# Group 0's first set of products on x as loaded, with paced loads and a later conversion

## The chip, the cores and the metric

The kernel runs on one core of one Trainium2 chip. The metric is the device time of one execution, in microseconds (us). Three runs of the kernel before gave 512.93, 513.04 and 513.55, median 513.04. A core has TensorE (PE, matmuls), VectorE (DVE), ScalarE (ACT), GpSimd (POOL) and SyncE (SP, which here only issues DMA transfers). All data is float32.

## The reference

The input x has 2 x 1024 rows of 512. Every row is normalised, then goes two ways: through a masked linear layer, and through a gated feed-forward with 1792 inner features whose output gates the first.

```
xn = (x - mean) / sqrt(var + 1e-5)                    # per row of 512
s  = xn @ (weight * blockmask).T                      # 512 x 512, blocks of 32 x 32
nx = xn * rsqrt(mean(xn^2) + 1e-5) * ln_w
h  = silu(nx @ gate_w.T) * (nx @ up_w.T)              # 1792 inner features
g  = silu(h @ down_w.T)
out = x + s * g
```

## The kernel before, in words

**Seven products in two levels.** Every large product is done with a Strassen-like scheme: a product of 2 x 2 blocks takes 7 instead of 8 block products, with sums and differences of the blocks before and after. It is applied twice. The outer level (q = 1 to 7, in the order `OUTER`) splits the work into 7 sets; the inner level (m = 1 to 7) makes each set out of 7 products of a 128 x 128 weight by a 128 x 512 operand. A product appears in the profile as two matmul records.

**Groups and instances.** The gate and up weights form 7 groups g (128 rows of each half of both); an eighth group, `G`, is the masked linear layer. One pair (g, q) is an *instance* j of 7 products (`instance`, L333). The order is first (g, 1) and (g, 2) for all groups, then the other five sets of each. So instance 0 is group 0, q = 1; instance 1 is group 0, q = 2; instances 2 and 3 are group 1, q = 1 and 2. The sets q = 1 and 2 use the first 1024 tokens (token tiles t = 0 and 1, of 512 tokens); q = 1 uses features 0 to 255 (chunks c = 0, 1), q = 2 features 256 to 511 (c = 2, 3). The down projection follows the same way at the end (L591).

**An order written out by hand.** `at(pos, fn)` puts a step into one list that is sorted by `pos`; the steps are then issued in that order, so each engine's order, and that of the DMA queue on SP, is the order of the positions. A position is 0.86 us, one product. Instance j's products stand from 7j on; `EARLY` overrides some of the first. `T(us)` turns a planned time into a position. Each engine runs its own list in order; semaphores make it wait for what it needs.

**The opening.** SP loads four x tiles of 128 tokens for t = 0 (`load_x`, L121), the first weight blocks (`load_a`, L251), x for t = 1, and so on. One GpSimd copy (L685) holds the first weight load until the first x tile has landed. For t = 0 and then t = 1: VectorE makes mean and variance per token (`stats`, L125 and L126), `factors` makes scale and shift from them (VectorE, a square root on ACT, VectorE), `normalise` applies them to the four tiles, half on ACT (L148) and half on VectorE (L146), `transpose` turns 128 x 128 blocks on TensorE into PSUM banks (L155), and `evacuate` copies a bank of 128 features x 512 tokens to memory (`raw`, L163). Those are the operands m = 1, 2, 3 of an inner product; m = 5, 6, 7, 4 are differences of them (`inner_b`, L97, since all additions are made by the helper `add`). On the weight side `scale_a` multiplies a block by `ln_w` (L262 on GpSimd, L264 on ACT) and `inner_a` makes four sums of its 128 x 128 blocks. Until the first real transpose, TensorE multiplies the identity by itself (`warm`, L702, 26 products).

**Within an instance.** Products accumulate in PSUM banks X, Y, Z (`PSB`: 3, 2 and 1 of them, V has 2). `seed`, `snap` and `total` copy partial sums out or add them up: from the bank, with the sums of an earlier instance (`prior`) if there is one. For group 0, instance 0 writes its four results to `acc`, instance 1 adds to them and gives the first quadrant of gate and up, `c1`. `silu` (ACT) and `h_out` (VectorE) make h from it, at position `SILU` = 26.2 at the earliest. The `acc` tiles go out to `acc_dram` for the later sets (L466) at 15 positions after the instance's start, and come back before them (L467). The kernel is started in `kernel`, which lays out the arrays; `x_t` is x transposed, used for the final addition only.

Of the kernel before, what the change touches and what calls it, by code (L numbers as in the profile page):

```python
# [31 lines left out]
def tile_masked_linear_gated_ffn(  # L32
# [19 lines left out]
    h_dram = tc.dram_tile([7, G, 2, P, W], F32, name="h_dram")  # L52
    s_dram = tc.dram_tile([KC, NTT, P, W], F32, name="s_dram")
    rms_dram = tc.dram_tile([NT], F32, name="rms_dram")
    acc_dram = tc.dram_tile([G + 1, P, 4, W], F32, name="acc_dram")
    dw_dram = tc.dram_tile([4, P, G, 256], F32, name="dw_dram")

# [45 lines left out]
    ident = const.tile([P, P], F32, tag="ident", name="ident")  # L103
    blockones = const.tile([P, P], F32, tag="blockones", name="blockones")
    keep = const.tile([P, 4, 16], F32, tag="keep", name="keep")

    def constants():
        make_identity(nc, ident)
        nc.gpsimd.memset(blockones, 0.0)
        for b in range(P // BLK):  # L110
            nc.gpsimd.memset(blockones[b * BLK : (b + 1) * BLK, b * BLK : (b + 1) * BLK], 1.0)


    xt, raw, stat = {}, {}, {}
    agg = small.tile([P, NTT, TT, 2], F32, tag="agg", name="agg", bufs=1)
    rms = small.tile([P, NTT, TT], F32, tag="rms", name="rms", bufs=1)

    def load_x(t):
        for i in range(TT):
            xt[t, i] = mem[:, first_slot[("B6", "vc", "v5", "B4")[t]] + i, :]  # L120
            nc.sync.dma_start(xt[t, i], x[(t * TT + i) * P : (t * TT + i + 1) * P, :])  # L121

    def stats(t, i):
# [4 lines left out]
    def factors(t):  # L128


        scl = small.tile([P, TT], F32, tag="scl", name=f"scl_{t}")
        nb = small.tile([P, TT], F32, tag="nb", name=f"nb_{t}")
        stat[t] = (scl, nb)

        def last():
            nc.vector.reciprocal(scl, scl)
            nc.vector.scalar_tensor_tensor(nb, agg[:, t, :, 0], -1.0, scl, ALU.mult, ALU.mult)

        return [lambda: nc.vector.tensor_scalar(scl, agg[:, t, :, 1], 1.0 + EPS, EPS * EPS, ALU.mult, ALU.add),
                lambda: nc.scalar.activation(scl, scl, AF.Sqrt), last]  # L140
# [168 lines left out]
        k = keep[:, 2 * R + K, :].unsqueeze(2).to_broadcast([P, 16, BLK])  # L309
        nc.gpsimd.tensor_tensor(v, v, k, ALU.mult)  # L310

    def inner_a(g, part, k0=0, n=2):

        if part == 1:
            i, si, qs = F["a1"] + 2 * (g % 3), F["s"] + 2 * (g % 2), (1, 2)
        else:
            i, si, qs = *w_slots(g), BLOCKS
        a, s = slots(i + k0, n), slots(si + k0, n)
        a11, a21, a12, a22 = (a[:, :, k * P : (k + 1) * P] for k in range(4))
        s1, s2, s3, s4 = (s[:, :, k * P : (k + 1) * P] for k in range(4))  # L320
        for k in range(n):
            aop[g, qs[k0 + k]] = {1: a11[:, k], 2: a12[:, k], 3: s4[:, k], 4: a22[:, k],
                                  5: s1[:, k], 6: s2[:, k], 7: s3[:, k]}
        return [lambda: add(pool, s1, a21, a22), lambda: add(pool, s2, s1, a11, ALU.subtract),
                lambda: add(pool, s4, a12, s2, ALU.subtract), lambda: add(pool, s3, a11, a21, ALU.subtract)]

    def weights(g, q, m):
        if q < 3 and m in (1, 2, 4):
            return aq[g, 0, q - 1][:, {1: 0, 2: 2, 4: 3}[m] * P :][:, :P]
        return aop[g, q][m]  # L330


    def instance(j, g, q, prior, dest, after):  # L333
# [1 line left out]

        st = {}

        seeded = j > 1

        def mm(m, tag, key, first):  # L340
            if first and key not in st:
                st[key] = bank("Y" if key == "z" and j == 1 else tag, f"{key}_{j}")
            nc.tensor.matmul(st[key], weights(g, q, m), operand(q, m), start=first and not (key == "z" and seeded),  # L343
                             stop=True, skip_group_check=True)

        def seed():

            if seeded:
                st["z"] = bank("Z", f"z_{j}")
                nc.scalar.copy(st["z"], st["x"])  # L350
            else:
                st["s1"] = slot("s2" if j else "s5", f"s1_{j}")
                if prior is None:
                    nc.scalar.copy(st["s1"], st["x"])
                else:
                    add(dve, st["s1"], st["x"], prior(0))
# [15 lines left out]
            else:  # L372
                add(dve, dest(i), st[key], prior(i))

        at(EARLY.get((j, 0), 7 * j + 1), seed)
        for off, m, tag, first, snapshot, out in (
            (0, 1, "X", True, None, None),
            (2, 5, "Y", True, ("s5", 3), None),
# [5 lines left out]
        ):  # L384
            key, pos = tag.lower(), 7 * j + off
            at(EARLY.get((j, m), pos), mm, m, tag, key, first)
            if snapshot:
                at(pos + 1, snap, key, *snapshot)
            elif out:

                pos += 2.3 if prior is None and m == 2 and seeded else 1
                if m == 2:
                    pos = EARLY.get((j, "z"), pos)
                at(pos, total, key, *out)
                after(out[1], pos)


    def group(g, where):
# [39 lines left out]
        def summed(dst, src, into, then=None, engines=(pool,) * 4):  # L438
# [14 lines left out]
            3: (vc, vc, done(0, 1, vc)),  # L453
            4: (acc, acc, done(1, 0, acc)),
        }
        for q in setup:
            instance(where[g, q], g, q, *setup[q])

        def h_sum(q, n, tile_of, a, b):

# [2 lines left out]
            nc.sync.dma_start(h_dram[HD[q], g, n], o)  # L463

        sums, rest = slots(F["acc"] + 4 * (g % 2), 4), 7 * where[g, BLOCKS[0]]
        at(7 * where[g, 1] + 15, lambda: nc.sync.dma_start(acc_dram[g], sums))  # L466
        at(rest - (14 if g else 6), lambda: nc.sync.dma_start(sums, acc_dram[g]))  # L467
        if g < G:
            def again():
# [88 lines left out]
    def load_final(R, Hh, i, slot_s, slot_x):  # L558
# [3 lines left out]
        nc.sync.dma_start(fin[m, t][0], s_dram[m, t])  # L562
        s_tile = fin[m, t][0]
        at_later.append(lambda: nc.gpsimd.tensor_tensor(s_tile, s_tile, rms_bc[t], ALU.mult))  # L564
        nc.sync.dma_start(fin[m, t][1], x_t[m * P : (m + 1) * P, t * W : (t + 1) * W])

    def finish(R, Hh, i, y, pos, eng, part=slice(0, W), source=None):
        r, n = divmod(i, 2)
# [15 lines left out]
    def down_instance(o, q, where_, prior, dest, after):  # L584
# [78 lines left out]
        if last_set:  # L663
            at(where_(17) + 0.1, base_of_last)
            for part, pos in zip(parts, (where_(23), where_(24), where_(25))):
# [8 lines left out]
    where = {gq: j for j, gq in enumerate(order)}  # L674
    N = len(order)
    END = 7 * N
    T = lambda us: (us - 14.0) / 0.86
    EARLY.update({(0, 1): T(10.4), (0, 2): T(11.3), (1, 1): T(12.1), (1, 2): T(13.0), (0, 0): T(11.5), (1, 0): 4.3,
                  (0, "z"): 3.26, (1, "z"): 4.9})
    SILU = 26.2  # L680
    at(T(-10), constants)
    at(T(-10), load_x, 0)
    at(T(-10), lambda: nc.scalar.dma_start(lnw_sb, ln_w))

    at(T(-10), lambda: nc.gpsimd.tensor_copy(mem[:, F["a1"], 0:1], xt[0, 0][:, 0:1]))  # L685
    for K in range(2):
        at(T(-10), load_a, 0, K)
    at(T(-10), load_x, 1)
    for K in range(2):
        at(T(-10), load_a, 1, K)  # L690
    at(T(-10), load_x, 2)
    for K in range(2):
        at(T(-10), load_a, 2, K)
    at(T(-10), load_x, 3)
    def plan(pos, step, todo):
        for i, fn in enumerate(todo):
            at(pos + step * i, fn)
# [3 lines left out]
        for _ in range(n):  # L701
            nc.tensor.matmul(b[:, :P], ident, ident, start=True, stop=True, skip_group_check=True)  # L702

    at(T(1.4), lambda: warm(26, bank("V", "idle")))
    for t, p, step in ((0, T(7.1), 0), (1, T(12.5), 0), (2, 36.0, 1.2), (3, 36.1, 1.2)):
        plan(p, step, factors(t))
    for i in range(TT):
        half = act if i < 2 else dve
        at(T(3.7 + 0.82 * i), stats, 0, i)
        at(T(9.35 + 0.82 * i), stats, 1, i)  # L710
        for h, cols in enumerate((slice(0, W // 2), slice(W // 2, W))):
            at(T(7.95 + 0.9 * h + 0.4 * (i % 2)), normalise, 0, i, half, cols)
            at(T(13.45 + 0.9 * h + 0.4 * (i % 2)), normalise, 1, i, half, cols)
        for c in range(KC):
            at(T((8.9, 9.3, 9.8, 11.0)[c] + 0.05 * i), transpose, 0, c, (2, 3, 0, 1)[i], "XYYX"[c])
            at(T((14.35, 14.8, 15.25, 16.2)[c] + 0.05 * i), transpose, 1, c, (2, 3, 0, 1)[i], "XVVV"[c])
    at(T(6.0), scale_a, 0, 0, pool)
    at(T(6.1), scale_a, 0, 1, pool)
    for c in range(KC):
        at(T((9.75, 10.3, 10.85, 12.05)[c]), evacuate, 0, c, act)  # L720
        at((5.6, T(15.6), 6.0, 3.14)[c], evacuate, 1, c, act)
    for pos, q, m, eng in ((1.1, 1, 5, dve), (1.87, 1, 6, dve), (2.56, 1, 7, dve), (3.95, 2, 5, dve), (2.7, 1, 4, pool),
                           (4.6, 2, 6, dve), (7.2, 2, 7, dve), (5.0, 2, 4, pool)):
        at(pos, inner_b, q, m, eng)
    for q in (1, 2):
        for k in (0, 1):
            for n in (0, 1):
                at(8, outer_b, q, k, n, None)
    at(2.1, scale_a, 1, 0)
    at(5.2, scale_a, 1, 1)  # L730
    for i in range(TT):
        at(14.0 + 2.5 * i, stats, 2, i)
        at(25.0 + 3 * i, stats, 3, i)
        at((44.0, 51.0, 55.2, 58.2)[i], normalise, 2, i, act)
        at(40.5 + 2.4 * i, normalise, 3, i, dve)
    plan(36.2, 1.2, rms_factor())

    for t, p0 in ((3, 51.5), (2, 65.5)):
        n = t % 2
# [21 lines left out]
    for g in range(G + 1):  # L761
        p, rest = 7 * where[g, 1], 7 * where[g, BLOCKS[0]]
        for K in range(2):
# [3 lines left out]
                at(p - (10.4, 7.3)[K], lambda K=K: mask_a(aq[G, 0, K], 0, K))  # L767
            elif g > 1:
                at(p - (10.4, 7.3)[K], scale_a, g, K)
        if g:  # L770
            plan(p - 7, 1, inner_a(g, 1))
        else:
            plan(T(9.9), 0, inner_a(0, 1, 0, 1))
            plan(T(11.9), 0, inner_a(0, 1, 1, 1))
        at(rest - 29, load_block, g)

        def block_sums(g=g):
# [147 lines left out]
```

## Time and profile before

| what | us |
|---|---|
| median of three runs | 513.04 |
| the profiled execution's own time | 513.17 |
| its span, first to last instruction | 511.4 |
| TensorE busy | 505.8 (99%) |
| VectorE busy | 380.4 (74%) |
| GpSimd busy | 340.9 (67%) |
| ACT busy | 182.6 (36%) |
| first real transpose on TensorE starts | 10.16 |
| first product of instance 0 starts | 11.48 |
| first product of instance 3 starts | 31.14 |

All times in the profile are counted from the span's start. A timeline line gives the start, the length, the engine, the line of the kernel, the operation with what it writes and reads, the number of merged instructions, and in brackets how long the engine had been idle and what it had waited for. [...]

### The profile page before, as it was taken

Reading aid. Unit: us, or ns where it says so; the run is one execution under the profiler, and the core shown is the slowest. Engines: PE = TensorE matmul, PEld = TensorE weight load, DVE = VectorE, ACT = ScalarE, POOL = GpSimd, SP = SyncE. Lnnn points to the kernel's source line nnn. Section 1 sums busy time; section 2 is a strip of 40 time slices with the busy share of each in tenths; the row PEclk is TensorE's granted clock in tenths of the full one; section 3 lists DMA queues with packets and bytes.
Section 4 is the critical chain, followed back from the end, with each engine's and each line's share of the span. In section 5 each row is a group of like instructions: output and inputs, shape, how many; then the busy total and the mean of one; then the engine's idle time right before and its main releaser. Section 6 shows DMA issues by size and latency. Waiting matters only on the chain. (4 is left out here: it accounts for less than half of the span.)

```text
span 511.4 us, 4943 instructions
## 1 busy us (share of the span) xinstructions
PE 505.8 (99%) x1269; PEld 231.8 (45%) x1269; DVE 380.4 (74%) x590; ACT 182.6 (36%) x348; POOL 340.9 (67%) x283
## 2 busy tenths in 40 slices
PE   8999999999999999999999999999999999999997
PEld 8444444444444444444444444444444444444444
DVE  6878689876977969699696978968747645367736
ACT  4656754633536353353634433330100101001111
POOL 5522224994795968869597789976662754739960
PEclk9999999999999999999999999999999999999999
DMA  8436636369159386785948667499997698476472
GB/s 289 164 132 238 247 133 227 135 236 350 48 219 348 147 302 228 238 289 208 338 166 294 209 239 254 169 332 383 357 339 270 204 374 327 146 252 216 151 229 83
DMA packets 60460, 121.59 MB, mean 238 GB/s; under 512 B 5760, under 2 KB 13328, under 8 KB 58384
## 3 DMA queue, kind: packets, MB, share of 16 engines
q1 hardware_dynamic: 60288, 121.27, 66.8%
q8 instruction: 10, 0.16, 0.1%
q14 instruction: 18, 0.15, 0.1%
q10 hardware_dynamic: 144, 0.00, 0.0%
HBM read 75.11 MB, written 46.15 MB: 237 GB/s over the span
## 5 line engine op out<-in xcount | busy, mean ns | idle before, releaser
L97 POOL TENSOR_TENSOR mem<-mem 128x512 f32<-128x512 f32 (+4 forms) x245 | 305.2, 1267 | 135.4 <-ACT mem L264 36.5
L343 PE MATMUL x<-mem 128*128 128x512 f32 x448 | 213.6, 595 | 0.2 <-DVE mem L97 0.2
L343 PEld LDWEIGHTS x<-mem 128*128 128x128 f32 x448 | 83.7, 190 | 107.3 <-issue 86.9
L97 DVE TENSOR_TENSOR mem<-x,mem 128x512 f32<-128x512 f32 x137 | 92.5, 684 | 42.0 <-PE x L343 41.1
L343 PE MATMUL y<-mem 128*128 128x512 f32 x224 | 114.5, 593 | 0.3 <-DVE mem L97 0.3
L97 DVE TENSOR_TENSOR mem<-mem 128x512 f32<-128x512 f32 (+3 forms) x60 | 74.7, 1252 | 7.8 <-PE dx L591 4.3
L591 PE MATMUL dx<-mem 128*128 128x512 f32 x174 | 78.3, 592 | 0.0
L97 DVE TENSOR_TENSOR mem<-y,mem 128x512 f32<-128x512 f32 x96 | 65.6, 684 | 9.8 <-PE y L343 8.5
L343 PEld LDWEIGHTS y<-mem 128*128 128x128 f32 x224 | 42.2, 190 | 53.0 <-issue 47.8
L350 ACT COPY z<-x 128x512 f32<-128x512 f32 x54 | 30.9, 573 | 97.9 <-PE x L343 92.2
L343 PE MATMUL z<-mem 128*128 128x512 f32 x112 | 57.3, 593 | 0.0
L591 PEld LDWEIGHTS dx<-mem 128*128 128x128 f32 x174 | 33.1, 190 | 41.6 <-issue 40.4
L591 PE MATMUL dy<-mem 128*128 128x512 f32 x98 | 44.5, 592 | 0.0
L409 ACT ACTIVATE gate<-mem 128x512 f32<-128x512 f32 x56 | 33.1, 601 | 25.3 <-DVE mem L97 20.9
L414 DVE TENSOR_TENSOR mem<-gate,mem 128x512 f32<-128x512 f32 x56 | 38.0, 681 | 5.1 <-POOL mem L97 4.3
L564 POOL TENSOR_TENSOR mem<-mem 128x512 f32<-128x512 f32 x16 | 25.0, 1570 | 15.3 <-DMA mem<-s_dram 15.2
L343 PEld LDWEIGHTS z<-mem 128*128 128x128 f32 x112 | 21.0, 190 | 24.9 <-issue 23.9
L574 ACT ACTIVATE silu<-mem 128x512 f32<-128x512 f32 x15 | 9.0, 602 | 64.6 <-DVE mem L97 48.3
L97 DVE TENSOR_TENSOR mem<-z,mem 128x512 f32<-128x512 f32 x41 | 28.0, 682 | 3.5 <-PE z L343 3.5
L591 PEld LDWEIGHTS dy<-mem 128*128 128x128 f32 x98 | 18.6, 190 | 23.4 <-issue 23.4
L97 DVE TENSOR_TENSOR mem<-dx,mem 128x512 f32<-128x512 f32 x16 | 11.0, 690 | 20.1 <-PE dx L591 20.1
L591 PE MATMUL dz<-mem 128*128 128x512 f32 x56 | 25.2, 592 | 0.0
(73 smaller groups left out, 289.2 us busy)
## 6 DMA issues: line engine op xcount, KB each, us to landing
h_dram<-mem SPq DMA_DIRECT2D x98, 256.0 KB, 2.1
mem<-h_dram SPq DMA_DIRECT2D x28, 768.0 KB, 6.2
mem<-in_gu SPq DMA_DIRECT2D x42, 256.0 KB, 3.7
acc_dram<-mem SPq DMA_DIRECT2D x8, 1024.0 KB, 4.2
mem<-acc_dram SPq DMA_DIRECT2D x8, 1024.0 KB, 6.7
mem<-in_x SPq DMA_DIRECT2D x16, 256.0 KB, 5.2
s_dram<-mem SPq DMA_DIRECT2D x16, 256.0 KB, 4.8
mem<-s_dram SPq DMA_DIRECT2D x16, 256.0 KB, 6.3
```

What stands on the lines that cost most here:

```text
L97: eng.tensor_tensor(o, a, b, op)
L343: nc.tensor.matmul(st[key], weights(g, q, m), operand(q, m), start=first and not (key == "z" and seeded), stop=True, skip_group_check=True)
L350: nc.scalar.copy(st["z"], st["x"])
L409: nc.scalar.activation(gate[key], t(), AF.Silu)
L414: nc.vector.tensor_mul(a(), gate[key], b())
L564: at_later.append(lambda: nc.gpsimd.tensor_tensor(s_tile, s_tile, rms_bc[t], ALU.mult))
L574: nc.scalar.activation(b[0][:, part], y[:, part] if source is None else source(), AF.Silu)
L591: nc.tensor.matmul(st[key], w(), b(), start=first and key != "z", stop=True, skip_group_check=True)
```

## The change

Instance 0 no longer waits for normalised x. Normalising a token is a scale and a shift, so `(x * scale + shift) @ w = scale * (x @ w) + shift * (sum of w over the features)`. The change multiplies the raw `x_t`, loaded already transposed, and converts the four results later.

- **Raw operands.** `x_t` is laid out by chunk and token tile. `raw_x` loads four blocks of 128 features x 512 tokens; `raw_t` makes their differences 5 and 6 on VectorE, 7 and 4 on GpSimd. In `instance`, j = 0 takes these as operands, and its products are planned from 4.6 us on. The first weight block is scaled on ACT and its sums are made on VectorE. `warm` makes 5 instead of 26 idle products.
- **Paced loads.** The first fourteen loads are a list in a fixed order: the weight block for q = 1, four raw blocks, the four x tiles of t = 0, the weight block for q = 2, the four x tiles of t = 1. Loads 3 to 10 of it (counted from 0) each wait for a one-column VectorE copy that reads the tile loaded three places earlier.
- **The order of the opening.** t = 0 is normalised after the raw products, features 256 to 511 first; instance 1 and instances 2 and 3 start around that. The two halves of the weight block of q = 2 are scaled on ACT at 9.8 us in the plan, ahead of the root of `factors` for t = 0. The scaling of group 1's blocks moves from ACT to GpSimd. Position 0 is at 12.2 instead of 14.0 us.
- **Conversion.** `sum_rows` multiplies the scaled weights by a column of ones (the sum over the features). `fac_store` transposes the factors of t = 0 and 1 on TensorE, copies them on ACT, stores them and loads them back broadcast over the partitions. `raw_results` scales and shifts instance 0's results, and adds them to instance 1's: 12 GpSimd operations and 4 on ACT, from position 16 on. `silu` and `h_out` of this quadrant are at fixed positions, 31 and 33 for the first half, 44 and 46 for the second, and the store to `acc_dram` at 46.5.
- A root of a column of ones is taken in `constants`; instance 1 now uses bank Z and instance 2 bank Y; x of t = 1 has other slots; statistics of t = 2 and 3 come a few positions later.

```diff
-    def load_x(t):
-        for i in range(TT):
-            xt[t, i] = mem[:, first_slot[("B6", "vc", "v5", "B4")[t]] + i, :]
+    def load_x(t, *tiles):
+        for i in tiles or range(TT):
+            xt[t, i] = mem[:, (F["B6"], F["B3"] + 2, F["v5"], F["B4"])[t] + i, :]
...
+    def raw_x(k, n):
+        o = rop[k, n] = mem[:, RQ[2 * k + n], :]
+        nc.sync.dma_start(o, x_t[k, n])
+
+    def raw_t(m, eng):
+        b11, b12, b21, b22 = (rop[k, n] for k in (0, 1) for n in (0, 1))
+        o = rop[m] = mem[:, RQ[{5: 4, 6: 5, 7: 6, 4: 7}[m]], :]
+        a, b = {5: lambda: (b12, b11), 6: lambda: (b22, rop[5]), 7: lambda: (b22, b12), 4: lambda: (b21, rop[6])}[m]()
+        add(eng, o, a, b, ALU.subtract)
...
+    def sum_rows():
+        b = bank("V", "row_sums")
+        for r in range(2):
+            for c in range(2):
+                nc.tensor.matmul(b[:, r : r + 1], aq[0, 0, 0][:, (2 * c + r) * P :][:, :P], ones,
+                                 start=c == 0, stop=c == 1, skip_group_check=True)
+        held.append(b)
...
+    def fac_store():
+        b = bank("V", "fac_rows")
+        nc.tensor.transpose(b[: 4 * TT, :P], fac.rearrange("p a t i -> p (a t i)"), ident)
+        rows = small.tile([4 * TT, P], F32, tag="fac_rows", name="fac_rows", bufs=1)
+        nc.scalar.copy(rows, b[: 4 * TT, :P])
+        nc.sync.dma_start(fac_dram.rearrange("a t (i p) -> (a t i) p", p=P), rows)
+        for a in range(2):
+            for t in range(2):
+                nc.sync.dma_start(fac_bc(a, t), fac_dram[a, t].unsqueeze(0).to_broadcast([P, W]))
...
+    def raw_results(p1, c1, silu, h_out):
+
+        tmp = [mem[:, F["B7"] + k, :] for k in range(4)]
+
+        def shift(i):
+            r, n = divmod(i, 2)
+            nc.scalar.mul(tmp[i], fac_bc(1, n), row_sums[:, r : r + 1])
+
+        pos = CONVERT
+        for n in (0, 1):
+            for i in (n, n + 2):
+                at(pos + 0.5, shift, i)
+                at(pos, lambda i=i, n=n: add(pool, p1(i), p1(i), fac_bc(0, n), ALU.mult))
+                at(pos + 1.5, lambda i=i: add(pool, p1(i), p1(i), tmp[i]))
+                at(pos + 3, lambda i=i: add(pool, c1(i), c1(i), p1(i)))
+                pos += 4.5
+            at((31, 44)[n], *silu(n))
+            at((33, 46)[n], *h_out(n))
...
-    T = lambda us: (us - 14.0) / 0.86
...
+    T = lambda us: (us - 12.2) / 0.86
...
+    landing, queue = [], []
+    for o, load in ([(aq_slot(0, 0), lambda: load_a(0, 0))] +
+                    [(mem[:, RQ[2 * k + n], :], lambda k=k, n=n: raw_x(k, n)) for k, n in ((0, 0), (1, 0), (0, 1), (1, 1))] +
+                    [(mem[:, F["B6"] + i, :], lambda i=i: load_x(0, i)) for i in range(TT)] +
+                    [(aq_slot(0, 1), lambda: load_a(0, 1))] +
+                    [(mem[:, F["B3"] + 2 + i, :], lambda i=i: load_x(1, i)) for i in range(TT)]):
+        queue.append((o, load))
+
+    def paced(k):
+        if 3 <= k < 11:
+            dve.tensor_copy(queue[k][0][:, 0:1], queue[k - 3][0][:, 0:1])
+        queue[k][1]()
+
+    for k, us in enumerate((-10, -10, -10, 3.6, 4.2, 4.9, 5.72, 6.52, 7.15, 8.0, 8.8, 8.81, 8.82, 8.83)):
+        at(T(us), paced, k)
...
-    at(T(1.4), lambda: warm(26, bank("V", "idle")))
...
+    at(T(1.4), lambda: warm(5, bank("V", "idle")))
+
+    at(T(4.0), scale_a, 0, 0)
+    for us, m, eng in ((5.75, 5, dve), (6.55, 6, dve), (6.8, 7, pool), (6.7, 4, pool)):
+        at(T(us), raw_t, m, eng)
+    plan(T(4.95), 0, inner_a(0, 1, 0, 1, dve))
+    at(T(10.0), sum_rows)
+    at(T(14.4), lambda: nc.scalar.copy(row_sums, held[0][:, :2]))
+    at(T(18.3), fac_store)
...
+    at(T(9.8), scale_a, 0, 1)
+    plan(T(10.6), 0, inner_a(0, 1, 1, 1))
+    at(T(12.4), scale_a, 1, 0, pool)
+    at(T(12.5), scale_a, 1, 1, pool)
...
-        "x_t": x.reshape(B * S, H).T,
+        "x_t": x.reshape(-1, W, KC, P).transpose(2, 0, 3, 1),
```

## The prediction

> **What bounds the kernel now.** I read the engine table first, then TensorE's waits, its timeline in the first 32 us, the loads, and the busy time by stretches.
>
> ```profile
> PE 505.8 (99%) x1269; PEld 231.8 (45%) x1269; DVE 380.4 (74%) x590; ACT 182.6 (36%) x348; POOL 340.9 (67%) x283
> ```
>
> ```profile
> PE idle L702 <- POOL ident masks.py:199: 1.3, 1, 1.3
> PE y L343 <- DVE mem L97: 0.3, 1, 0.3
> PE x L343 <- DVE mem L97: 0.2, 1, 0.2
> ```
>
> ```profile
> 31.10:503.00 471.90, 471.75 (x1122) 1.00 0.68 241
> ```
>
> TensorE never waits after its first 22 us: from 31.1 to 503 it is busy 471.75 of 471.90 us. So the time is set by when that gapless stretch begins. The mark I use is the first product of instance 3 (group 1, q = 2); what TensorE does from there on is the same in both kernels.
>
> ```profile
> 1.35 8.98 PE L702 MATMUL idle<-ident 128*128 128x128 f32 x52 [1.35 <-POOL ident masks.py:199]
> 10.16 1.47 PE L155 MATMUL pt<-ident,mem 128*128 128x128 f32 x12
> 11.48 1.10 PE L343 MATMUL x<-mem 128*128 128x512 f32 x2
> ...
> 13.72 1.02 PE L343 MATMUL x<-mem 128*128 128x512 f32 x2
> ...
> 31.14 1.45 PE L343 MATMUL x<-mem 128*128 128x512 f32 x3
> ```
>
> A product is two records, 0.86 us from start to start. The mark is at **31.14**. Between 11.48 and 31.14 lie 19 products (16.3 us), 20 transposes at 0.11 (2.2) and 1.1 us of small gaps: this stretch is nearly full too. Only the 9 us of idle products (L702) ahead of it can be used.
>
> ```profile
> 6.00:7.00 1.00, 1.00 (x6) 1.00 1.04 389
> 8.00:9.00 1.00, 1.00 (x11) 1.00 0.95 358
> ```
>
> The columns are the stretch, its length, PE busy (records), granted clock, DMA share, GB/s. TensorE passes 6 idle records in the seventh microsecond and 11 in the ninth; the single records start every 0.213 us until 7.5, every 0.111 after. For 6 us from its first record it ran at half speed, which the PEclk row doesn't show.
>
> [...] The trace has 2.5 to 3.4 for loads not behind a long queue (below). [...]
>
> **The change, part by part.**
>
> *The seven raw products.* The set q = 1 of group 0 (7 products, 6.0 us at full clock, twice that at half) goes to where the idle products were. It needs the first weight block scaled: load landed 3.54 (as the first x load today, issue 0.73), `lnw_sb` landed 3.7, two ACT halves 0.91: first product at 4.8. Five idle products (10 records x 0.213 from 1.45) end at 3.8, so TensorE then idles 1 us and is still cold. [...] (0,1) 4.8, (0,2) 6.5, (0,5) 8.2, (0,6) 9.5, (0,3) 10.4, (0,7) 11.2, row sums 12.1 (four products of one column, 8 records at 0.11 to 0.19; I take 0.9), (0,4) to 13.9[...]. All of it lies before the transposes below, so the cold clock costs nothing unless loads are faster than I take them.
>
> *Paced loads.* From the fourth on, a load waits for a VectorE copy that waits for the landing three loads earlier. So at most three are under way, and one round costs issue to landing plus 0.26 us (0.02 to the copy, 0.18 copy, 0.05 to the issue: today's gate, POOL L685, 3.67 to 3.85, issue at 3.88). What is a landing worth?
>
> ```profile
> L251 SPq DMA_DIRECT2D mem<-in_gu x1: 328/328/328, 3.9 to 3.9; - x1
> ...
> DMA to landing us min/median/max: 3.4/3.4/3.4
> ```
>
> ```profile
> L251 SPq DMA_DIRECT2D mem<-in_gu x6: 332/352/400, 41.6 to 68.3; - x6
> ...
> DMA to landing us min/median/max: 2.5/2.8/3.1
> ```
>
> The first is today's gated load in the opening, 3.4 us; the second is six weight loads with one or two under way, 2.5 to 3.1; the very first x load took 2.8. With three under way I take **2.9**, and keep 2.5 and 3.4 as ends. The new plan's own gate times (3.6, 5.72, 8.0) imply 2.0; no load in this trace was that fast, and the old plan's time for scaling that gated block was 6.0, where the trace has 7.50. Ungated, today's queue lands a load every 0.67 us; gated, three per 3.16, so one per 1.05.
> The chain that matters is loads 0, 3, 6, 9 (load 9 is the block for q = 2): 3.54 + 3 x 3.16 = **13.0**. x's fourth tile (load 8) lands at 11.2, its statistics end at 12.2.
>
> *Behind that landing on ACT.* `scale_a(0, 1)` stands on ACT ahead of the square root and the normalising, so those wait for load 9: two scaling halves (0.82 to the next start), root 0.2, reciprocal and shift on VectorE 0.4: normalising of tiles 0 to 3 starts at 13.0 + 1.5 = **14.5**, where today it starts at 7.8.
>
> *From there (times after 14.5).* ACT: four halves at 0.5, to 2.0, then two evacuations (0.5 apart) end at 2.6 and 3.1. Products (1,1) at 2.7, (1,2) at 3.6 to 4.4; eight transposes to 5.1; evacuation to 5.7; (2,1) 5.75 to 6.6. VectorE meanwhile: two normalisings (0.5 each), four statistics (0.81 each), one total (0.6), ready for the second factors at 5.0; ACT's root comes after the evacuation, 5.6, factors at 6.2. (2,2) 6.6 to 7.5. New here: `fac_store` puts a transpose behind (2,2) on TensorE and its copy on ACT ahead of three of the four normalising halves, so ACT stands from 6.9 to 7.8; the halves run 8.0 to 9.6. Transposes 8.7 to 9.4, first difference on VectorE 0.7, and (1,5) at **9.9**. Then 8 products (6.86), 8 transposes (0.88) and three changes of kind at 0.08 to the mark: 9.9 + 7.9 = **17.8**; 14.5 + 17.8 = **32.3**, against 31.14. That is **+1.2 us**. TensorE idles where it used to be full: the work freed early is paid back as gaps between 14 and 25 us.
>
> *GpSimd's conversion.* 12 additions of 128x512 at 1.28 are 15.4 us, with the four for group 2 (0.73) between them. They can begin once the broadcast factors are in (store about 22.5, 2 us, loads 2.6 more) and the group 1 difference is done, about 29, and end near 47. The later gates (positions 31 and 44) come at about 40 and 52, and the next GpSimd results are needed at 52: 3 us of cover. GpSimd is busy only 2.9 of each 12.8 us there today. I cost it at nothing; each microsecond beyond that cover would be one of TensorE.
>
> *The rest.* Two more ACT copies, four shifts (0.57 each) and VectorE's 8 gates (0.18), two differences (0.68) and four weight sums (0.3) lie where those engines wait anyway. Scaling of group 1 moves from ACT (0.91 a block) to GpSimd (1.86), done by 20, needed at 20. SP's four raw loads add 1 MB of 122; the factor store and its loads hold SP about 2 us near 23, where its next load of today is at 25.5. The final x loads keep packets and size. Banks and slots: nothing.
>
> **Sum.** 513.17 (the profiled execution: span 511.4 and 1.8 around it; 0.13 above the median) + 1.2 = **514.3**. A measurement of this kernel tells about 0.2% (1.03 us, so 512.0 and 514.07) from no change.
>
> **Rivals.**
> *The loads land like today's middle ones*, 2.6 us: load 9 at 12.1, mark at 31.4: 513.4, no change. [...] against: 3.4 in the opening. 0.30.
> *The plan holds*: loads of 2.0 us. Then the clock decides: VectorE's total of (0,7) stands ahead of the reciprocal. With the clock full by 7.5 us, (0,7) ends near 11.2, normalising starts at 12.1, mark 29.9: 511.9, faster. With a switch at 9.1 it starts at 13.2, and nothing is won. 0.18.
> *Every gated load takes 3.4*, as today's: load 9 at 14.5, mark 33.8: 515.8, clearly slower; it decides from 2.8 us a load (mark at 32.04). 0.16.
> My forecast has the other 0.36. GpSimd late by more than its cover would add to any of them.
>
> **How the numbers follow.** Slower by over 0.2%: most of the forecast (0.28), the 3.4 case (0.16), a little of the 2.6 case (0.03): 0.47. Within: 0.36. Faster: 0.17, from the plan's case. The range from 511.7 to 515.9 leaves out about half of each outer case.
>
> **What would show it.** In the new trace: first product near 4.8 and two cold products of 1.7 us; gated loads 2.5 to 3.4 from issue to landing; ACT's scaling of the second block near 13 and the first normalising near 14.5; TensorE idle between 13.9 and 24; the mark at 32.3; no waits after it. I am wrong if loads land in about 2 us, if ACT's normalising doesn't wait for the second block, or if TensorE waits for GpSimd between 40 and 55 us.

## The result and the profile after

The changed kernel takes **516.75 us** (median of four runs, 516.66 to 517.02; the kernel before 513.08 beside them). The ratio is 1.0071 with a 95% interval of 1.0053 to 1.0088: slower by 0.7%, 3.7 us. I had forecast slower by 1.2. The profiled execution took 516.68 us with a span of 514.9, where before it was 513.17 and 511.4.

I split the 3.5 us between the two spans at two points that both kernels have: the mark (first product of instance 3) and the start of TensorE's last matmul record (507.36 and 509.85), called the last product's start below.

| stretch, us | before | after | more | I had predicted |
|---|---|---|---|---|
| start to the mark | 31.14 | 32.87 | 1.73 | 1.2 |
| mark to the start of the last product | 476.23 | 476.99 | 0.76 | 0 |
| start of the last product to the end | 4.03 | 5.04 | 1.01 | not looked at |

**The engine table** answers to the first fence of the prediction: fewer matmuls, the same busy time; ACT and GpSimd do more.

```profile
PE 505.9 (98%) x1236; PEld 227.6 (44%) x1236; DVE 383.0 (74%) x598; ACT 186.5 (36%) x358; POOL 357.4 (69%) x293
```

**TensorE's waits** grow from 1.8 us in three places to 3.9 in seven, all in the opening; the largest:

```profile
PE idle L794 <- POOL ident masks.py:199: 1.4, 1, 1.4
PE x L397 <- DVE mem L98: 0.8, 2, 0.7
PE pt L164 <- ACT mem L157: 0.6, 1, 0.6
```

**TensorE's timeline in the opening**, columns as in the prediction:

```profile
1.38 2.50 PE L794 MATMUL idle<-ident 128*128 128x128 f32 x10 [1.38 <-POOL ident masks.py:199]
4.43 2.06 PE L397 MATMUL x<-mem 128*128 128x512 f32 x2 [0.55 <-ACT mem L273]
6.28 1.92 PE L397 MATMUL z<-mem 128*128 128x512 f32 x2
...
13.46 1.13 PE L397 MATMUL x<-mem 128*128 128x512 f32 x2 [0.66 <-DVE mem L98]
14.71 1.90 PE L164 MATMUL pt<-ident,mem 128*128 128x128 f32 x8
16.49 2.08 PE L397 MATMUL x<-mem 128*128 128x512 f32 x2
18.35 1.24 PE L397 MATMUL z<-mem 128*128 128x512 f32 x2
...
32.87 1.45 PE L397 MATMUL x<-mem 128*128 128x512 f32 x3
```

The raw products run from 4.43, the first two at half speed, as forecast. The forecast's times for them suppose full speed from 9.1 us, an estimate of mine that the trace of the kernel before (full from 7.47) did not show; here it began at 8.54. The product at 16.49 was not forecast like this: from its start to the next is 1.86 us, as at 4.43 (1.85), though TensorE had been at full speed since 8.54. The busy time by stretches shows the granted clock in its fourth column:

```profile
8.40:11.80 3.40, 3.40 (x8) 1.00 0.83 278
11.80:15.20 3.40, 2.62 (x14) 1.00 1.02 269
15.20:18.60 3.40, 3.40 (x9) 0.52 0.86 316
```

For 3.41 us, from 15.37 to 18.78 in the clock record, TensorE was back at half speed. In the 3.41 us before, it had idled about 0.8 us and otherwise done one product, eight products of one column, and transposes.

**ACT at the hand-over** from the loads to the normalising, with the last gated load (the weight block of q = 2) below it:

```profile
12.40 0.91 ACT L273 ACTIVATE mem<-mem,lnw_sb 128x256 f32<-128x256 f32 x2 [1.63 <-DVE st L131]
13.21 0.19 ACT L149 ACTIVATE fac<-fac 128x4 f32<-128x4 f32 x1
13.89 2.08 ACT L157 ACTIVATE mem<-mem,fac 128x256 f32<-128x256 f32 x4 [0.49 <-DVE fac L146]
```

```profile
L260 SPq DMA_DIRECT2D mem<-in_gu x1: 328/328/328, 9.7 to 9.7; - x1
...
DMA to landing us min/median/max: 2.6/2.6/2.6
```

Issued at 9.69, landed at 12.31, scaled at 12.40, normalised from 13.89: the chain of the prediction, 0.6 us earlier. (The scaling's label names VectorE's statistics, which ended at the same moment. In all eight profiles with gates the scaling starts 0.08 to 0.09 us behind load 9's landing.)

**After the mark** the stretch still looks full:

```profile
32.80:504.80 472.00, 471.70 (x1121) 1.00 0.69 243
```

Yet TensorE has two late products, in the timeline around 44 and 56 us. The gaps show in no idle column: a product's records are longer than the distance to the next product (1.02 against 0.86 us at 39.73), so the start-to-start distance must be read.

```profile
42.31 1.88 PE L397 MATMUL x<-mem 128*128 128x512 f32 x4
44.20 1.10 PE L397 MATMUL y<-mem 128*128 128x512 f32 x2
45.14 1.88 PE L397 MATMUL x<-mem 128*128 128x512 f32 x4
```

Two products should take 1.72; here they take 1.89, and the next one 0.94 instead of 0.86. What ACT does just before, and then ACT and the product in the kernel before:

```profile
39.94 0.57 ACT L404 COPY z<-x 128x512 f32<-128x512 f32 x1 [1.13 <-PE x L397]
40.52 1.28 ACT L483 ACT_TABLE_LOAD   x1
41.82 0.60 ACT L483 ACTIVATE gate<-mem 128x512 f32<-128x512 f32 x1
42.35 0.71 ACT L458 ACTIVATE mem<-mem,row_sums 128x512 f32<-128x512 f32 x1
42.97 0.58 ACT L483 ACTIVATE gate<-mem 128x512 f32<-128x512 f32 x1
43.49 0.57 ACT L415 COPY mem<-y 128x512 f32<-128x512 f32 x1
```

```profile
39.21 0.60 ACT L409 ACTIVATE gate<-mem 128x512 f32<-128x512 f32 x1 [0.44 <-DVE mem L97]
39.92 0.58 ACT L361 COPY mem<-y 128x512 f32<-128x512 f32 x1
...
42.30 1.02 PE L343 MATMUL y<-mem 128*128 128x512 f32 x2
```

The copy of bank y (`snap`, L415) must end before the next product into y. Before, it ended at 40.50, and that product came at 42.30. After, four instructions queue back to back ahead of it: the silu's table load (at 32.84 in the kernel before), the silu, a shift copy of the conversion (L458) and another silu. It ends at 44.06, and the product starts at 44.20. The same happens at 56.64 behind the second half's silu. Neither time does ACT wait for GpSimd.

**The tail.** The last two stores of the output, before and after:

```profile
L578 SPq DMA_DIRECT2D out<-mem x2: 403/404/406, 508.3 to 508.8; - x2
...
DMA to landing us min/median/max: 1.7/1.8/1.8
```

```profile
L658 SPq DMA_DIRECT2D out<-mem x2: 332/360/387, 511.1 to 511.6; - x2
...
DMA to landing us min/median/max: 2.4/2.5/2.6
```

They take 0.7 us longer, and the first is issued 0.3 late behind a wait of SP. The trace has an 8 KB transfer of an instruction queue (q14) at 512.5, between issue and landing of both. It ends at 512.9, and only then do the last 18 packets of the stores begin; in each of the seven profiles where this transfer falls on the stores, these packets begin within 0.01 us of its end. SP's wait comes 1.4 us ahead of the transfer. Both come and go together in all profiles, but what ties them is not shown. In the kernel before that transfer came at 512.3, 0.9 us after the span's end.

### The profile page after: what moved, and what is told of

Its sections match the earlier page's. It is cut to its first block, busy times and chain, and to the rows that moved or that the text cites. A ratio compares the mean times of both kernels' runs of the same rounds, so it can differ in the third digit from the quotient of the medians.

```text
span 514.9 us, 4925 instructions
## 1 busy us (share of the span) xinstructions
PE 505.9 (98%) x1236; PEld 227.6 (44%) x1236; DVE 383.0 (74%) x598; ACT 186.5 (36%) x358; POOL 357.4 (69%) x293
## 5 line engine op out<-in xcount | busy, mean ns | idle before, releaser
L98 POOL TENSOR_TENSOR mem<-mem 128x512 f32<-128x512 f32 (+4 forms) x255 | 321.8, 1285 | 124.7 <-ACT mem L425 32.3
L397 PE MATMUL x<-mem 128*128 128x512 f32 x448 | 216.2, 600 | 1.7 <-DVE mem L98 0.8
L98 DVE TENSOR_TENSOR mem<-x,mem 128x512 f32<-128x512 f32 x134 | 90.5, 684 | 38.9 <-PE x L397 38.1
L98 DVE TENSOR_TENSOR mem<-mem 128x512 f32<-128x512 f32 (+2 forms) x66 | 78.3, 1194 | 7.4 <-PE dx L671 4.4
L397 PE MATMUL z<-mem 128*128 128x512 f32 x112 | 58.4, 604 | 0.0
```

Source lines behind the costliest of these rows:

```text
L98: eng.tensor_tensor(o, a, b, op)
L397: nc.tensor.matmul(st[key], weights(g, q, m), operand(q, m) if j else rop[{1: (0, 0), 2: (1, 0), 3: (1, 1)}.get(m, m)], start=first and no ...
```

## The experiments

Each is the changed kernel with one edit or more; ratios are to the kernel before. "Normalising", "mark", "to last" and "tail" are ACT's first normalising half, the mark, the mark to the last product's start, and from there to the end, in the profiled execution.

| kernel | median us | ratio, 95% interval | normalising | mark | to last | tail |
|---|---|---|---|---|---|---|
| the changed kernel | 516.75 | 1.0071 [1.0053, 1.0088] | 13.89 | 32.87 | 476.99 | 5.04 |
| `fill` | 517.37 | 1.0078 [1.0063, 1.0093] | 14.21 | 33.32 | 477.39 | 5.07 |
| `ungated` | 513.96 | 1.0016 [1.0008, 1.0023] | 13.20 | 31.06 | 476.91 | 4.13 |
| `fac_late` | 517.24 | 1.0086 [1.0069, 1.0103] | 14.23 | 32.00 | 477.36 | 5.16 |
| `no_convert` | 515.33 | 1.0044 [1.0029, 1.0059] | 13.83 | 31.69 | 476.24 | 5.18 |
| `pad8` | 516.93 | 1.0072 [1.0057, 1.0087] | 14.91 | 32.78 | 477.20 | 5.10 |
| `ungated_shift` | 513.50 | 1.0004 [0.9996, 1.0013] | 12.93 | 30.79 | 476.51 | 4.13 |
| `ungated_order` | 513.70 | 1.0010 [1.0001, 1.0018] | 13.40 | 31.76 | 476.48 | 4.13 |
| `fill_shift` | 516.81 | 1.0078 [1.0060, 1.0095] | 14.32 | 32.19 | 476.97 | 5.13 |
| `pad_sp` | 515.74 | 1.0042 [1.0027, 1.0057] | 14.76 | 32.63 | 477.23 | 4.12 |
| `ungated_order2` | 512.85 | 0.9990 [0.9983, 0.9998] | 12.12 | 30.43 | 476.52 | 4.14 |
| `ungated_order3` | 513.08 | 0.9997 [0.9990, 1.0004] | 11.92 | 30.13 | 476.50 | 4.13 |
| `after_shift` | 516.55 | 1.0062 [1.0041, 1.0084] | 14.92 | 33.55 | 476.37 | 5.05 |

### `fill`: keep TensorE busy where it idled

```diff
-    at(T(1.4), lambda: warm(5, bank("V", "idle")))
+    idle = []
+    at(T(1.4), lambda: idle.append(bank("V", "idle")))
+    at(T(1.4), lambda: warm(7, idle[0]))
+    at(T(10.05), lambda: warm(5, idle[0]))
+    at(T(10.9), lambda: warm(2, idle[0]))
```

> TensorE is kept from standing idle between the raw set and the first transposes: 7 idle products at the start, 5 more behind the row sums and 2 ahead of the last raw product's successors. If the second half-speed spell (15.2 to 18.6 us) comes from TensorE's idle moments in the window before it, it is gone, and the mark (first product of instance 3) comes about 1.2 us earlier, near 31.7, the time near 515.5. If the spell has nothing to do with idling, or the stretch is bound by VectorE and ACT anyway, the mark stays at 32.9 and the time at 516.7.

Not faster: 517.37. In its profile the clock stays full from 5.68, and (1,1) and (1,2) take their 0.9 us. But the time was not won: in this profile another wait took its place:

```profile
31.11 0.72 ACT L458 ACTIVATE mem<-mem,row_sums 128x512 f32<-128x512 f32 x1 [2.51 <-DMA mem<-fac_dram]
31.73 0.57 ACT L415 COPY mem<-y 128x512 f32<-128x512 f32 x1
```

```profile
32.35 1.12 PE L397 MATMUL y<-mem 128*128 128x512 f32 x2 [0.98 <-ACT mem L415]
```

ACT's first shift copy waits 2.51 us for the broadcast factors. The snap of y stands behind it on ACT, and TensorE waits 0.98 us for the snap. The store of the factors took 3.7 us to land here, 1.4 to 3.1 in the other profiles; in the changed kernel's the same copy waits 0.65 us, and TensorE not at all.

### `ungated`: the loads as one queue

```diff
-        if 3 <= k < 11:
-            dve.tensor_copy(queue[k][0][:, 0:1], queue[k - 3][0][:, 0:1])
...
-    for k, us in enumerate((-10, -10, -10, 3.6, 4.2, 4.9, 5.72, 6.52, 7.15, 8.0, 8.8, 8.81, 8.82, 8.83)):
-        at(T(us), paced, k)
+    for k in range(14):
+        at(T(-10), paced, k)
```

> The eight gates are taken out and all loads are issued in the same order at once. If the gates set the start of normalising (load 9 at 12.3 us), load 9 lands at about 9.7 and the normalising starts 1 us or more earlier; VectorE's total of the sixth raw product, which waits for the cold TensorE until about 12, is then the next bound, so the mark gains 0.8 to 1 us and the time is near 515.8. If the gates help the first loads, the first product (4.43) comes later and nothing is won.

The gates are the largest cost: 2.8 us come back (513.96), more than I expected. The loads land every 0.67 us, load 9 at 10.62 instead of 12.31, and the mark is at 31.06. From normalising to mark it takes 17.86 us. In the profiles 1.8 us of the gain lie ahead of the mark (0.7 an earlier normalising, 1.1 the half-speed spell) and 0.9 in the tail, now 4.13. The gates do not help the first loads: without them the first product starts at 4.36, with them at 4.43.

### `fac_late`: the factor store behind the transposes

```diff
-    at(T(18.3), fac_store)
+    at(T(19.66), fac_store)
```

> The store of the factors, its transpose on TensorE and its copy on ACT come behind the normalising of t = 1 instead of amid it. If ACT's standing there (22.0 to 22.85 us) delays the transposes of t = 1, product (1,5) comes 0.8 us earlier (24.9 to 24.1), and the mark and the time with it (516.0). If the transposes wait for VectorE, nothing changes. The conversion begins up to 1 us later; if GpSimd had no cover, stalls of TensorE between 40 and 57 us would grow.

No gain: 517.24. The first product of t = 1, (1,5), comes 9.0 us after the normalising, where `ungated`, with the old place of the store, has 9.9. But (2,3) then waits 0.45 us for ACT's snap behind the shift copy, as in `fill`, so the stretch to the mark is 17.77. The stretch after the mark is 1.1 us longer than before the change; that is not due to this move, for `fill`, without it, has 1.2.

### `no_convert`: no conversion

It leaves out the conversion: the 12 GpSimd operations and ACT's four shift copies. Instance 1 adds to the unconverted results, and the first quadrant of group 0 comes from them, with silu at its earlier position.

```diff
-            setup.update({1: (None, p1, nothing), 2: (None, c1, nothing)})
+            setup.update({1: (None, p1, nothing), 2: (None, c1, done(0, 0, c1))})
...
-            raw_results(p1, c1, lambda n: (silu, (0, 0, n), lambda: c1(n)),
-                        lambda n: (h_out, (0, 0, n), lambda: c1(n), lambda: c1(n + 2), n))
```

> The 12 GpSimd operations and 4 ACT copies of the conversion are left out, and silu and the product of this quadrant stand at their earlier gates: the first quadrant of group 0 is computed from unconverted results. Only what the conversion and its gates cost is taken away. If the stalls of TensorE after the mark (0.67 us at 44.2, 47.7 and 56.6) come from them, they are gone and the time is near 516.0; if they come from the shifted position of other work, they stay and the time is 516.7.

From the mark to the last product it takes 476.24 us, as before the change (476.23): the whole 0.76 is the cost of the conversion and of the later silu. (The profiles of `pad8` and `pad_sp`, the same kernel up to its end, have 0.97 and 1.00 there.) The opening shows no half-speed spell, and normalising to mark is 17.87.

### `pad8` and `pad_sp`: the tail

```diff
+    pad = small.tile([P, 1], F32, tag="pad", name="pad", bufs=1)
+    for k in range(8):
+        at(END + 40 + 2 * k, lambda: nc.vector.memset(pad, 0.0))
```

> Eight one-column VectorE memsets of an unused tile are added in the last stage; nothing else changes. If the last microsecond (5.0 us from the last product's start to the end, against 4.0 before) comes from an 8 KB instruction fetch that falls on the last stores, because VectorE has eight instructions more than before, eight more move that fetch ahead of the stores, and the stretch is 4.0 to 4.2 again: time near 515.8. If the stores are slow for another reason (the layout of x, the addresses), it stays at 5.0 and 516.8.

Eight more VectorE instructions changed nothing: 516.93, tail 5.10. Then the same with SP, eight transfers of 2 KB:

```diff
+    pad = small.tile([P, 8, KC], F32, tag="pad", name="pad", bufs=1)
+    for k in range(8):
+        at(END + 10 + 3 * k, lambda k=k: nc.sync.dma_start(pad[:, k, :], ln_w))
```

> The changed kernel with eight more small transfers (2 KB each, of the ln_w vector into an unused tile) in SP's queue in the last stage. Eight more VectorE instructions didn't move the last instruction fetch (2.7 us after the last product's start, on top of the last two stores). If it is SP's own instruction stream, which is nine transfers and eight waits longer than before, eight more transfers move that fetch ahead of the last stores' data: the stretch from the last product's start to the end is then 4.0 to 4.2 us again and the time 0.9 us shorter, 515.9. If the fetch is another engine's or isn't the cause, the stretch stays at 5.0.

More work, and 1.0 us faster: 515.74, tail 4.12. No instruction transfer falls on the output stores, and they are quick again. This page counts four stores; the last two landed 1.8 and 1.7 us after their issue.

```profile
L658 SPq DMA_DIRECT2D out<-mem x4: 333/391/406, 509.9 to 511.3; - x4
...
DMA to landing us min/median/max: 1.7/1.9/2.1
```

### `ungated_shift` and `after_shift`: ACT's queue

Shift copies where ACT is free, and the second half's silu, gate product and store later; once on `ungated`, once on the changed kernel as it is.

```diff
-                at(pos + 0.5, shift, i)
+                at({0: 17.1, 2: 20.9, 1: 24.1, 3: 26.1}[i], shift, i)
...
-            at((31, 44)[n], *silu(n))
-            at((33, 46)[n], *h_out(n))
+            at((31, 46.9)[n], *silu(n))
+            at((33, 48.5)[n], *h_out(n))
...
-        at(7 * where[g, 1] + 15 if g else 46.5, lambda: nc.sync.dma_start(acc_dram[g], sums if g else slots(R1, 4)))
+        at(7 * where[g, 1] + 15 if g else 49.0, lambda: nc.sync.dma_start(acc_dram[g], sums if g else slots(R1, 4)))
```

(On `ungated` the first position was 16.5.)

> Without the gates, and with the ACT copies of the conversion at positions 16.5, 20.9, 24.1 and 26.1 (the last at 30 so far), and the second silu, its product and the store behind it 2.5 positions later. If the stalls of TensorE after the mark (0.68 us at positions 34, 38 and 48) come from these ACT steps standing ahead of ACT's copies of product sums, they shrink to 0.1 or less and the time is near 513.3. If they come from GpSimd being late, they stay and the time is 514.0.

> The changed kernel with its gates and its opening, and only ACT's shift copies and the second half's silu, gate product and store at other positions. Theory (the stalls between 44 and 57 us are ACT's queue, with the gates as without them): from the mark to the last product's start about 476.5, where the changed kernel has 476.99, so 0.5 us less: about 516.2. The tail is left as it is, about 5.1. The opening is the same, so the run also tells whether the second half-speed spell belongs to this opening or comes by chance: if it belongs to it, TensorE's clock is at half in some 3.4 us between 15 and 19 again and the first product of instance 3 starts at about 32.9; if it is chance, that product may start at 31.7 (normalising at 13.9 and 17.8 behind it). Rival: the stalls are GpSimd's late conversion, and stay: 477.0 and 516.7.

With all 12 GpSimd operations in place, the stretch after the mark falls from 476.91 to 476.51 on `ungated` and from 476.99 to 476.37 on the changed kernel. So most of the stall is ACT's queue, not GpSimd. The median of `after_shift` moved by less than its interval. In its profile the opening was worse (mark 33.55). Here the half-speed spell came again, from 15.67 to 19.09, after nearly 2 us of waiting in the 3.41 us before:

```profile
13.84 1.13 PE L397 MATMUL x<-mem 128*128 128x512 f32 x2 [1.22 <-DVE mem L98]
15.74 1.97 PE L164 MATMUL pt<-ident,mem 128*128 128x128 f32 x8 [0.77 <-DVE mem L155]
17.53 1.88 PE L397 MATMUL x<-mem 128*128 128x512 f32 x2
```

### `ungated_order`, `ungated_order2`, `ungated_order3`: what an open queue allows

All three start from `ungated_shift`. The first takes VectorE's total of (0,7) behind the factors of t = 0, (0,4) behind it, and lets GpSimd make raw difference 7 ahead of 4.

```diff
-    ... (0, 4): T(10.8), ... (0, ("out", 7)): T(10.68), ...
+    ... (0, 4): T(13.45), ... (0, ("out", 7)): T(12.7), ...
...
-    for us, m, eng in ((5.75, 5, dve), (6.55, 6, dve), (6.8, 7, pool), (6.7, 4, pool)):
+    for us, m, eng in ((5.75, 5, dve), (6.55, 6, dve), (6.6, 7, pool), (6.7, 4, pool)):
```

> As the one before, and VectorE's total of product (0,7) comes behind the normalising of t = 0 instead of ahead of the reciprocal, product (0,4) behind the first transposes, and GpSimd makes the difference that (0,7) needs first. If, with the gates gone, the cold TensorE holds the normalising back through that total, the normalising starts near 11.6 (13.2 so far), the mark comes near 29.5 and the time near 511.8, faster than before the change. If another thing binds (ACT's scaling of the second block, the loads), it gains half a microsecond or nothing.

It missed: the normalising started at 13.40. GpSimd's difference, now at 7.28, fell on VectorE's second one:

```profile
6.57 2.52 DVE L98 TENSOR_TENSOR mem<-mem 128x512 f32<-128x512 f32 x2 [0.73 <-DMA mem<-in_x_t]
9.01 0.68 DVE L131 BATCH_NORM_STATS2 st<-mem 128x6 f32<-128x512 f32 x1
```

```profile
7.28 1.26 POOL L98 TENSOR_TENSOR mem<-mem 128x512 f32<-128x512 f32 x1 [5.16 <-DMA mem<-in_x_t]
```

```profile
6.70 1.42 DVE L98 TENSOR_TENSOR mem<-mem 128x512 f32<-128x512 f32 x2 [0.86 <-DMA mem<-in_x_t]
```

The last fence is `ungated`: the same two differences take 1.42 us there, 2.52 here, and the statistics slide by 1 us. Nothing else differs on VectorE at that time. The one that met GpSimd took 1.79 us, the other 0.69.

The second leaves that swap out, and scales the block of q = 2 on GpSimd (`scale_a, 0, 1, pool`); first shift copy at 17.1. The third adds the edit of `fac_late`.

> As the ungated run with the moved ACT copies (the first now at 17.1), and the total of (0,7) behind the normalising, (0,4) behind the first transposes, GpSimd's two raw differences in their old order (in the run before, the swapped one ran beside VectorE's and made that one 1.1 us longer), and the second block scaled on GpSimd, off ACT's queue. If the total and that scaling held the normalising back once the loads are free, it starts near 11.8 and the mark comes near 29.7: 511.9. If VectorE's statistics bind, it starts at 12.5 and the time is near 512.7. Nothing won at 513.5.

> As ungated_order2, with the store of the factors behind the normalising of t = 1. In the run with that alone, product (1,5) came 0.8 us earlier against the start of the normalising. If that adds up, the mark is 0.6 to 0.8 us ahead of ungated_order2's; if ACT's wait for the factors then stops a product sum, part of it is lost again.

`ungated_order2` is the one version faster than the kernel before: by 0.35 us, 0.10% with an interval of 0.02 to 0.17%. Its normalising starts at 12.12. VectorE makes the factors at 11.21, at once behind its last statistics, so the statistics bind now, and 512.85 is near the 512.7 expected for that case. So the idea is worth a little, once its waits are gone; what each of the edits gave was not separated. `ungated_order3` had a mark only 0.3 us earlier, and its median shows no gain.

### `fill_shift`: are the factors the next bound?

`fill` with the first shift copy at position 17.1, behind the snap of y.

> The kernel with the idle products in TensorE's gaps, and the conversion's first ACT copy moved behind ACT's copy of instance 2's sum, from position 16.5 to 17.1. In the fill run that first copy waited 2.5 us on ACT for the broadcast factors, and product (2,3) waited 1.0 us on TensorE behind it. If that is the second bound under the half-speed spell, the wait of 1.0 us is gone and the mark is near 32.3 (33.3 in fill, 32.9 in the changed kernel). If it is not, the mark stays at 33.3.

The 1 us wait is gone (mark 32.19, and 17.87 from normalising). The median is 516.81, 0.6 below `fill` with overlapping intervals, and not below the changed kernel. So being rid of the spell, which neither filled profile has, did not lower the median; see below.

## Why the prediction was right in direction and short in size

The step that failed is the one from the mark to the end. The prediction moved the mark by 1.2 us and added nothing behind it, since what TensorE does from there on "is the same in both kernels" and the conversion was costed "at nothing". In the profiled execution 1.77 of the missing 2.4 us lie behind the mark: 0.76 in stalls behind ACT and 1.01 in the last stores. The opening was short by 0.57.

**Paced loads: right.** I took 2.9 us a load and 14.5 for the normalising. The three gated loads of the chain took 2.74, 2.73 and 2.63 us, so load 9 landed at 12.31, not 13.0, and the normalising started at 13.89. That is one profile. Over the eight profiles with gates these loads took 2.5 to 3.6 us, mean 2.88, and the start lies between 13.83 and 14.92, mean 14.38. So this profile, with a mean of 2.70, lies nearer to the first rival's 2.6 than to my 2.9, and the eight together do not. What the trace of the kernel before has for that rival is two of its six weight loads between 41 and 69 us, those issued at 67.35 and 68.28, which landed after 2.63 and 2.49. `ungated` confirms that the gates set the normalising's start, though statistics and the total of (0,7) are close behind: there the block lands 1.7 us earlier and the normalising starts only 0.7 earlier.

**From normalising to the mark: right, with an addition.** My 17.8 is 17.86 or 17.87 in the six profiles without a half-speed spell, a factor wait or a reordered total. In the changed kernel's own it was 18.98. In that profile the failing sentence is "the cold clock costs nothing". It looked only at the first switch. TensorE idles behind the gates, as I had written ("TensorE idles where it used to be full"), and the clock falls back for 3.41 us: (1,1), (1,2) and eight transposes at half speed, 1.1 us. The step was mis-sized by that, not in its list of instructions. The spell came in two of the six gated profiles without fillers, in neither of the two with them, and in none of the five without gates. What decides whether it comes was not isolated.

The clocks of the other runs say more. Each run has its mean granted clock on record. A spell of 3.41 us at half speed takes 0.0033 off it (half of 3.41 in 515), and the fall of the clock behind the last work took off at most 0.0026 in the profiles. So 0.996 or less marks a run with a spell, and 0.998 or more one without. Of the changed kernel's four runs only the profiled one (0.996) had it; the other three, at 0.998 to 1.000, took 516.66, 516.83 and 517.02. So the spell belongs to the split of the profile and does not explain the median. What made those three as long was not profiled: a late normalising (`pad8`, no spell, 14.91 and a mark at 32.78) and a wait for the factors (`fill`) are two ways that other profiles show. Nor does the spell need the gates. Six of 20 runs of `ungated_order` have 0.996, with a median of 514.6 against 513.3 for the other 14. None of the eight runs with fillers has it.

Over the five gated profiles with the loads, products and factor store as in the changed kernel (its own, `no_convert`, both pads, `after_shift`) the mark lies between 31.69 and 33.55, mean 32.70; my 32.3 is 0.4 short of that.

**"I cost it at nothing", of the conversion and the later silu: wrong, 0.76 us.** I counted GpSimd's 15.4 us against 3 us of cover, and that held: its last conversion addition ended at 48.85, and the second half's silu ran at 55.40, behind other work of ACT. What failed is the sentence on the rest, that ACT's copies and shifts "lie where those engines wait anyway". On ACT the silu brings a table load of 1.28 us to 40.52, and silu and shift stand ahead of snaps that free a bank. `no_convert` has none of the 0.76, `after_shift` 0.14 of it. I had named a wait for GpSimd between 40 and 55 us as what would prove me wrong: the place was right, the engine was not.

**No step looked at the tail: 1.01 us.** I wrote that what TensorE does from the mark on "is the same in both kernels" and took the end as fixed to it. An 8 KB instruction transfer moved onto the last stores. Eight more transfers of SP moved it away (`pad_sp`, 4.12), eight more VectorE instructions did not (`pad8`, 5.10). All five kernels without gates have 4.13 or 4.14; there the transfer starts 0.3 to 0.5 us behind the stores' last packet. This part of the gates' cost is one of place, not of work.

**The sum.** I forecast 514.3, the profile gave 516.68. The 2.4 us between are the opening 0.57 (18.98 for 17.8, +1.18; normalising at 13.89 for 14.5, -0.61), the stalls 0.76 and the tail 1.01, but for rounding. This split is the profiled execution's; the runs behind the median may mix the opening's parts otherwise. Of the rivals, the one with 3.4 us a load gives about the right time (515.8) for a wrong reason: no load of the chain took 3.4 in this profile. The plan's 2.0 was not reached either.

## What to carry to other kernels

A gate on a load cost its latency for each round here: with three in flight the loads came at 250 to 270 GB/s in stretches of 4 us, from the open queue at up to 393. The order of the queue alone was enough. When work is moved, list for every engine what now stands ahead of the copies that free a bank, table loads included; a GpSimd budget alone is not enough. And look at the two ends of the trace separately: a microsecond lost in the last stores, or won by padding, says nothing of the idea.

## What the runs showed of the hardware

- **The clock fell back for 3.41 us without a long idle gap.** Twice it fell, at 15.37 and 15.67; the longest gap ahead was 1.22 us. The amount of waiting does not sort the cases: the 3.41 us before the first fall had 0.79 us of it, while ahead of their first transposes `pad_sp` waited 1.1 and `ungated_order` 1.13 us and neither fell back (mean clocks of 1.000 and 0.999). The columns that passed do sort the three that can be counted. An estimate from the records, each counted for the part that lies in the stretch, gives about 1490 and 1030 columns in the 3.41 us before the two falls, and about 1820 in `ungated_order` from 12.51 to 15.93. That order was found afterwards; no run tests it.
- **Full speed first began at different times**: at 5.68 us in `fill`, 7.47 in the kernel before, 8.54 in the changed kernel, and near 10.0 in `fac_late` (an estimate from the distances of its products). So one profile of an opening is a sample, and openings are compared by their stretches.
- **An 8 KB instruction transfer on the last stores came with 0.9 to 1.1 us more at the end** (tails of 5.04 to 5.18 against 4.12 to 4.14), and with eight idle transfers of 2 KB it no longer fell there (4.12). Where it fell on them, the stores' last 18 packets began within 0.01 us of its end.
- **A 128x512 difference on VectorE beside one on GpSimd took 1.79 instead of 0.69 us** (`ungated_order`).
